# First attention of a gated two-layer block: projections and statistics one step further ahead of the scores

## The chip, the core and the metric

The kernel runs on one core of a Trainium2 chip. Its engines are called as in the profile: PE (TensorE, the matmuls; PEld is its weight load), DVE (VectorE), ACT (ScalarE), POOL (GpSimd) and SP (SyncE, which issues most DMAs). The metric is the device time of one execution in microseconds (us); the number given for the kernel is the median of three runs.

## The reference, cut to what matters

`x` is 16 batches x 128 tokens x 256. Two layers follow, each an attention and a feed-forward part added to `x` through a tanh gate. Only the first attention is touched:

```python
ln_out = _ln(layernorm(x), ln_w, ln_b)
q = _fp8_linear_pertensor(ln_out, wq, wq_scale, q_in_scale)   # 16 heads x 128
q = _ln(q per head); k = _ln(fp8 linear, 8 heads); v = fp8 linear, 8 heads
core = gqa(q, k, v)                       # softmax(q k^T / sqrt(128)) v, 2 query heads per key head
qx = _ln(fp8 linear of ln_out, per head); kx, vx = split(ctx @ w_kv_x.T); kx = _ln(kx)
xout = gqa(qx, kx, vx)
catq = fp8 rounding of concat(core, xout) / proj_smooth
x = x + tanh(g) * (catq @ wproj.T) * scale
```

Inputs of a linear are scaled, clipped and rounded to an 8-bit float. The attention is computed in two passes: self (core) for all 16 batches, then cross (xout).

## The kernel before, in words

One batch in one pass is a `Unit`: `units[0..15]` self, `units[16..31]` cross. The work of a unit is cut into four steps of four query heads each. One loop over steps n from -11 to 135 (L626) issues for each n the pieces of several units; a table of lags, written out by hand in the loop's body (L627 to L665), says which piece of which unit belongs to step n. `do(n, lag, name)` calls a piece for the head group n - lag; `once(n, step, name)` calls it once per unit, when n - step is four times the unit's number; `front(n, i)` (L619) says which of a unit's eight projection blocks (two K, four Q, two V, each 128 tokens x 512) are due in step n.

For unit u, before the change:

- `stats` (every fourth unit, L290) and `prep_norm`, `prep_tr` at 4u-8, `prep_scale`, `prep_round` at 4u-7, `prep_last` at 4u-6: layer norm of x, transposition, scaling (POOL, L366), rounding (four DVE operations at L215 to L221, last subtraction on POOL at L227), store of the rounded cross input (L388);
- `project` (PE, L410), `evict` (ACT copy to a `raw` tile, L422, or to the value tile `vt`, L419) and `bn` (DVE, L431) of blocks 0 and 1 at 4u-5, 2 and 3 at 4u-4, 4 and 5 at 4u-3, 6 and 7 (values, no `bn`) at 4u-2;
- `rstd` at 4u-2: the reciprocal deviation of all 24 heads, by four small DVE operations (L438 to L443), Ln and Exp on ACT (L175, L176), and four more on DVE (L177 to L180);
- `mult` of both K blocks and of the first Q block at 4u-2 (POOL, L454), of the other Q blocks one step later each;
- `heads` one step behind `mult`: PE transposes (L463), ACT evicts to `kT` or `qT` (L472);
- `scores` (PE, L481), `top` (DVE, L489), `exp` (ACT, L497) for head group c at 4u+c; `recip` and `divide` (DVE L505, POOL L509) one step later, `probs` (PE L517, ACT L519) two, `values` and `smooth` (PE L527, DVE L538) three, `quant` (DVE, as in `prep_round`, for two groups at once) three, `quant_last` (POOL L227) four, `output` (PE L565) five; `residual` (DVE L579) at 4u+8.

Each tile tag has a fixed number of buffers: `raw` nine, `vt` two, `qT`, `kT`, `eT` two, `e` three; a tile is reused when its last reader is done. Weights come in pieces through `load_split` and `load_kvx` on SP, at steps given by `at` (L594 to L605): the slots of the self weights are reused for the cross weights once the last self unit has been projected.

The instruction order on each engine is fixed when the program is built. A planner takes the pieces in the order of the program as priorities, with its own costs of the instructions, and lets a later piece go ahead on an engine that it holds to be idle: in the trace, all six multiplications of a unit often stand in a row on POOL, and two layer norms of the feed-forward part run at 661 and 768 us, within the first attention. [...]

Of the kernel before, what the change touches and what calls it, by code (L numbers as in the profile page):

```python
# [9 lines left out]
F32 = mybir.dt.float32  # L10
# [8 lines left out]
P = 128  # L19
B = 16  # L20
# [11 lines left out]
K_Q, K_K, K_V, K_QX = 0, 1, 2, 3  # L32
# [3 lines left out]
def flamingo_kernel(  # L36
# [197 lines left out]
    NU = 2 * B  # L234
# [4 lines left out]
    with (  # L239
# [50 lines left out]
        def stats(g):  # L290

            xg = ap.tile([P, 4, DM], F32, tag="xg", name="xg", bufs=1)
            nc.sync.dma_start(
                out=xg, in_=x_in[4 * g : 4 * g + 4].rearrange("b s d -> s b d")
            )
            mv = small.tile([P, 4, 2], F32, tag="mv0", name="mv0", bufs=2)
            for j in range(4):
                stx = small.tile([P, 6], F32, tag="st0", name="st0")
                nc.vector.bn_stats(stx, xg[:, j, :])
                nc.vector.bn_aggr(mv[:, j, :], stx)  # L300
            v1 = small.tile([P, 4], F32, tag="v1", name="v1", bufs=1)
            nc.vector.tensor_scalar(v1, mv[:, :, 1], EPS, None, ALU.add)
            r1 = rsqrt(small, v1, 4, "x1", 1)
            v2 = small.tile([P, 4], F32, tag="v2", name="v2", bufs=1)
            nc.vector.tensor_tensor(v2, r1, r1, ALU.mult)
            nc.vector.tensor_tensor(v2, v2, mv[:, :, 1], ALU.mult)
            nc.vector.tensor_scalar(v2, v2, EPS, None, ALU.add)
            r2 = rsqrt(small, v2, 4, "x2", 1)
            rr = small.tile([P, 4], F32, tag="rr", name="rr", bufs=2)
            nc.vector.tensor_tensor(rr, r1, r2, ALU.mult)  # L310
            for j in range(4):
                norms[4 * g + j] = (xg[:, j, :], mv[:, j, 0:1], rr[:, j : j + 1])

        class Unit:
# [98 lines left out]
            def evict(self, blk):  # L413
                pm = self.pm.pop(blk)
                if blk >= 6:
                    if blk == 6:
                        self.vt = ap.tile([P, 1024], F32, tag="vt", name="vt")
                    c = blk - 6
                    nc.scalar.copy(self.vt[:, c * 512 : (c + 1) * 512], pm)  # L419
                    return  # L420
                raw = ap.tile([P, 4, P], F32, tag="raw", name="raw", bufs=9)
                nc.scalar.copy(raw.rearrange("p h d -> p (h d)"), pm)  # L422
                self.raws[blk] = raw

# [166 lines left out]
        def at(n, f, *args):  # L591
            loads.setdefault(n, []).append((f, args))

        for c in range(2):  # L594
            at(-8, load_split, K_K, wkT, c)
            at(-6, load_split, K_Q, wqT, c)
            at(-5, load_split, K_Q, wqT, c + 2)
            at(-4, load_split, K_V, wvT, c)
            at(4 * B - 8 + c, load_kvx, c, 0)
            at(4 * B - 7 + c, load_split, K_QX, wqxT, c)  # L600
            at(4 * B - 6 + c, load_split, K_QX, wqxT, c + 2)
            at(4 * B - 4 + c, load_kvx, c, 1)
        for q in range(4):
            at(-2 + q // 2, load_proj, 0, q)
            at(4 * B + 2 + q, load_proj, 1, q)  # L605
# [1 line left out]
        def do(n, lag, name, *args):  # L607

            m = n - lag
            if 0 <= m < 4 * NU:  # L610
                getattr(units[m // 4], name)(m % 4, *args)

        def once(n, step, name, *args):

            m = n - step
            if m % 4 == 0 and 0 <= m // 4 < NU:
                getattr(units[m // 4], name)(*args)

        def front(n, i):  # L619

            m = n + 5
            u, step = m // 4, m % 4
            return (units[u], 2 * step + i) if 0 <= u < NU else None

        first, last = -11, 4 * NU + 7
        for n in range(first, last + 1):  # L626
            for m in range(0, B, 4):  # L627
                if n == 4 * m - 11:
                    stats(m // 4)
            once(n, -8, "load")  # L630
            for f, args in loads.get(n, ()):
                f(*args)
            ab = [front(n, i) for i in range(2)]
            do(n, 1, "recip")
            do(n, 4, "quant_last")
            do(n, 1, "divide")
            do(n, 0, "scores")
            do(n, 2, "probs")
            do(n, 0, "top")
            do(n, 0, "exp")  # L640
            if ab[0]:
                ab[0][0].project(ab[0][1])
                ab[0][0].evict(ab[0][1])
            once(n, -6, "prep_last")
            do(n, 3, "values")
            do(n, 3, "smooth")
            if ab[0]:
                ab[0][0].bn(ab[0][1])
            once(n, -2, "rstd")
            for blk in range(2):  # L650
                once(n, -2, "mult", blk)
                once(n, -1, "heads", blk)
            do(n, -2, "mult_q")
            do(n, -1, "heads_q")
            do(n, 3, "quant")
            if ab[1]:
                ab[1][0].project(ab[1][1])
                ab[1][0].evict(ab[1][1])
                ab[1][0].bn(ab[1][1])
            do(n, 5, "output")  # L660
            once(n, 8, "residual")
            once(n, -8, "prep_norm")
            once(n, -8, "prep_tr")
            once(n, -7, "prep_scale")
            once(n, -7, "prep_round")  # L665

    G = 4
    NT = G * P
# [408 lines left out]
    for g in range(B // G):  # L1077
# [3 lines left out]
        for b in range(g * G, (g + 1) * G):  # L1081
# [8 lines left out]
    ap = f2.enter_context(tc.tile_pool(name="a1", bufs=2, side="right", reuse_waits="tile"))  # L1090
    psum = f2.enter_context(
        tc.tile_pool(
            name="psum1", bufs=1, space=bass.MemoryType.PSUM, reuse_waits="tile"
# [6 lines left out]
    for n in range(-2, N1 + 5):  # L1100
# [14 lines left out]
        m = n + 2  # L1115
# [7 lines left out]
        m = n - 4  # L1123
# [5 lines left out]
    for stages in routes:  # L1129
        for _ in stages:  # L1130
# [6 lines left out]
            name="psum2", bufs=2, space=bass.MemoryType.PSUM, reuse_waits="tile"  # L1137
# [6 lines left out]
    for e in range(NE):  # L1144
# [21 lines left out]
        for c in range(NCC):  # L1166
            po = ps_sc([P, DM])
            for f in range(NFC):
# [11 lines left out]
                    ap=xe[:, c, 2 * DM + 1 : 2 * DM + 2].bitcast(I32), axis=0  # L1180
# [79 lines left out]
```

## Time and profile before

| | |
|---|---|
| median of three runs | 1548.32 us (1547.97 to 1548.7) |
| the profiled execution's own time | 1546.6 us |
| its span, first to last instruction | 1544.9 us |
| granted PE clock, mean | 0.969 |
| first scores of the first attention | at 64 us |
| self units 1 to 13 | 84.3 to 453.8 us |
| cross units 17 to 29 | 543.4 to 888.0 us |
| end of the first attention | about 948 us |
| busy over the span: PE, DVE, ACT, POOL | 90%, 68%, 53%, 43% |

The page gives for each engine its busy time and share of the span. A view by stretches gives the same for any part of the span. The list of waits says, for each group of instructions, how long its engine sat idle before it and which instruction's end ended that; the view in order of time shows the instructions with their start, length and, in brackets, the idle time before them and its releaser. The chain that ended last covers only the final scatter of this program (its longest piece is 10 us of issue at the very end), so the stages have to be read one by one.

### The profile page before, as it was taken

Reading aid. Unit: us, or ns where it says so; the run is one execution under the profiler, and the core shown is the slowest. Engines: PE = TensorE matmul, PEld = TensorE weight load, DVE = VectorE, ACT = ScalarE, POOL = GpSimd, SP = SyncE. Lnnn points to the kernel's source line nnn. Section 1 sums busy time; section 2 is a strip of 40 time slices with the busy share of each in tenths; the row PEclk is TensorE's granted clock in tenths of the full one; section 3 lists DMA queues with packets and bytes.
Section 4 is the critical chain, followed back from the end, with each engine's and each line's share of the span. In section 5 each row is a group of like instructions: output and inputs, shape, how many; then the busy total and the mean of one; then the engine's idle time right before and its main releaser. Section 6 shows DMA issues by size and latency. Waiting matters only on the chain. (4 is left out here: it accounts for less than half of the span.)

```text
span 1544.9 us, 24676 instructions
## 1 busy us (share of the span) xinstructions
PE 1395.5 (90%) x8628; PEld 1008.7 (65%) x8628; DVE 1053.4 (68%) x2789; ACT 813.6 (53%) x2420; POOL 670.8 (43%) x574
## 2 busy tenths in 40 slices
PE   2778889798888999999999987999999999996998
PEld 1567677677776677777777774555556666664887
DVE  8988878878788777776767764433579796983100
ACT  3666566566566676666666662442445554551121
POOL 4566666666666655555565654120021312111111
PEclk9799999999999999999999998999999999996999
DMA  4300001000013100000000005300210100001562
GB/s 122 112 6 23 24 11 35 12 11 21 11 45 99 45 26 16 12 21 11 18 15 18 8 8 145 104 1 0 78 54 9 49 8 36 9 36 62 191 198 70
DMA packets 50764, 68.69 MB, mean 44 GB/s; under 512 B 4939, under 2 KB 37387, under 8 KB 50640
## 3 DMA queue, kind: packets, MB, share of 16 engines
q1 hardware_dynamic: 36640, 41.31, 9.0%
q10 hardware_dynamic: 11376, 17.63, 3.5%
q0 software_dynamic: 2624, 8.16, 1.5%
q8 instruction: 69, 1.13, 0.3%
q14 instruction: 55, 0.45, 0.1%
HBM read 50.53 MB, written 16.81 MB: 44 GB/s over the span
## 5 line engine op out<-in xcount | busy, mean ns | idle before, releaser
L509 POOL TENSOR_TENSOR e<-e,sums 128x512 f32<-128x512 f32 x128 | 139.9, 1093 | 230.5 <-DVE sums L505 120.7
L497 ACT ACTIVATE e<-ps_sc,mx 128x128 f32<-128x128 f32 x512 | 181.4, 369 | 89.6 <-DVE mx L489 82.2
L454 POOL TENSOR_TENSOR raw<-raw,q_r 128x512 f32<-128x512 f32 x192 | 208.6, 1116 | 34.5 <-DVE q_r L180 33.3
L431 DVE BATCH_NORM_STATS2 q_st<-raw 128x6 f32<-128x128 f32 x768 | 173.9, 278 | 66.6 <-ACT raw L422 66.3
L1013 ACT ACTIVATE e<-ps_sc,mx 128x128 f32<-128x128 f32 x512 | 139.7, 384 | 119.7 <-DVE mx L1004 114.7
L565 PE MATMUL ps_acc<-wp,cat 128*128 128x512 f32 x512 | 160.4, 436 | 17.7 <-POOL cat L227 15.5
L463 PE MATMUL ps_tr<-ident,raw 128*128 128x128 f32 x768 | 120.7, 285 | 46.0 <-POOL raw L454 43.8
L227 POOL TENSOR_TENSOR cat<-e_t,e_e 128x1024 fp32r<-128x1024 bf16 x64 | 136.3, 2129 | 53.6 <-DVE e_t L221 53.6
L481 PE MATMUL ps_sc<-kT,qT 128*128 128x128 f32 x1024 | 138.6, 278 | 14.9 <-ACT qT L472 14.9
L481 PEld LDWEIGHTS ps_sc<-kT,qT 128*128 128x128 f32 x1024 | 129.3, 191 | 33.0 <-ACT qT L472 27.1
L463 PEld LDWEIGHTS ps_tr<-ident,raw 128*128 128x128 f32 x768 | 95.1, 146 | 82.9 <-POOL raw L454 57.9
L519 ACT COPY eT<-ps_tr 128x512 f32<-128x512 f32 x128 | 75.4, 589 | 139.5 <-PE ps_tr L517 139.4
L968 POOL TENSOR_TENSOR kb<-kT,hmask 128x512 f32<-128x512 f32 x32 | 33.6, 1069 | 250.3 <-PE ps_sc L997 188.3
L565 PEld LDWEIGHTS ps_acc<-wp,cat 128*128 128x128 f32 x512 | 95.9, 194 | 57.5 <-POOL cat L227 22.2
L527 PE MATMUL ps_pv<-eT,vt 128*128 128x256 f32 x512 | 132.1, 379 | 1.0 <-DVE cat_y L538 1.0
L422 ACT COPY raw<-ps_mm 128x512 f32<-128x512 f32 x192 | 113.8, 594 | 28.8 <-PE ps_mm L410 26.1
L527 PEld LDWEIGHTS ps_pv<-eT,vt 128*128 128x128 f32 x512 | 95.8, 189 | 31.2 <-issue 9.0
L538 DVE TENSOR_TENSOR cat_y<-ps_pv,r_sm 128x512 bf16<-128x512 f32 x128 | 87.0, 680 | 39.6 <-PE ps_pv L527 39.4
L472 ACT ACTIVATE qT<-ps_tr,hv 128x512 f32<-128x512 f32 x128 | 101.0, 789 | 21.2 <-PE ps_tr L463 19.3
L497 ACT ACTIVATION_READ_ACCUMULATOR e<-ps_sc,mx 128x1 f32 x512 | 105.6, 206 | 0.0
L489 DVE TENSOR_REDUCE mx<-ps_sc 128x4 f32<-128x512 f32 x128 | 87.2, 681 | 23.3 <-PE ps_sc L481 23.2
L1004 DVE TENSOR_REDUCE mx<-ps_sc 128x8 f32<-128x1024 f32 x64 | 78.2, 1221 | 26.1 <-PE ps_sc L997 24.5
(227 smaller groups left out, 2818.5 us busy)
## 6 DMA issues: line engine op xcount, KB each, us to landing
w1t<-in_w ACTq DMA_DIRECT2D x8, 1024.0 KB, 6.4
w2t<-in_w ACTq DMA_DIRECT2D x8, 1024.0 KB, 5.4
disp<-empty SPq DMA_DIRECT2D x16, 257.0 KB, 9.8
xe<-disp SPq DMA_DIRECT2D x8, 514.0 KB, 3.7
stage<-in_wprojT SPq DMA_DIRECT2D x16, 256.0 KB, 2.7
xg<-in_x SPq DMA_DIRECT2D x4, 512.0 KB, 3.9
xb<-in_x SPq DMA_DIRECT2D x16, 128.0 KB, 2.0
ctx<-in_ctxT SPq DMA_DIRECT2D x16, 128.0 KB, 2.2
```

What stands on the lines that cost most here:

```text
L227: nc.gpsimd.tensor_tensor(dst, t[:, part], e[:, part], ALU.subtract)
L422: nc.scalar.copy(raw.rearrange("p h d -> p (h d)"), pm)
L431: nc.vector.bn_stats(self.st[:, 4 * blk + j, :], self.raws[blk][:, j, :])
L454: nc.gpsimd.tensor_tensor(src, src, self.r[:, 4 * blk : 4 * blk + 4, None].to_broadcast([P, 4, P]), ALU.mult,)
L463: nc.tensor.transpose(pt[:, j, :], src[:, j, :], ident)
L472: nc.scalar.activation(dst, pt, AF.Identity, scale=hv[:, col : col + 1], bias=hv[:, col + 1 : col + 2])
L481: nc.tensor.matmul(pscore[:, j, :], qT[:, j, :], self.kT[:, 2 * c + j // 2, :], start=True, stop=True,)
L497: nc.scalar.activation(e[:, j, :], pscore[:, j, :], AF.Exp, bias=self.mx[:, j : j + 1], accum_out=sums[:, j : j + 1],)
L509: nc.gpsimd.tensor_tensor(e, e, sums[:, :, None].to_broadcast([P, 4, P]), ALU.mult)
L527: nc.tensor.matmul(pv[:, 2 * g : 2 * g + 2, :], self.vt[:, gg * P : (gg + 1) * P], eT[:, 2 * g : 2 * g + 2, :], start=True, stop=True,)
L565: nc.tensor.matmul(self.acc, self.cat[c // 2][:, h % 8, :], wpr[self.cross, c][:, j, :, :], start=(h == 0), stop=(h == 15),)
L1013: nc.scalar.activation(e[:, i, :], s[:, i // NQ, i % NQ, :], AF.Exp, bias=mx[:, i : i + 1])
```

## The change

Everything up to `rstd` is done one step earlier relative to the scores: `front` uses n + 6 in place of n + 5, all `prep_` pieces, `load`, `stats`, `rstd` and the weight loads of `at` move by one step, and the loop starts at -12. `mult`, `heads` and all that follows stay where they were; so do the loads of the output projection's weights (`load_proj`). Since the projected blocks and the values now live a step longer, `raw` gets eleven buffers and `vt` three: 8 KB more per partition.

```diff
-                        self.vt = ap.tile([P, 1024], F32, tag="vt", name="vt")
+                        self.vt = ap.tile([P, 1024], F32, tag="vt", name="vt", bufs=3)
...
-                raw = ap.tile([P, 4, P], F32, tag="raw", name="raw", bufs=9)
+                raw = ap.tile([P, 4, P], F32, tag="raw", name="raw", bufs=11)
...
-            at(-8, load_split, K_K, wkT, c)
-            at(-6, load_split, K_Q, wqT, c)
-            at(-5, load_split, K_Q, wqT, c + 2)
-            at(-4, load_split, K_V, wvT, c)
-            at(4 * B - 8 + c, load_kvx, c, 0)
-            at(4 * B - 7 + c, load_split, K_QX, wqxT, c)
-            at(4 * B - 6 + c, load_split, K_QX, wqxT, c + 2)
-            at(4 * B - 4 + c, load_kvx, c, 1)
+            at(-9, load_split, K_K, wkT, c)
+            at(-7, load_split, K_Q, wqT, c)
+            at(-6, load_split, K_Q, wqT, c + 2)
+            at(-5, load_split, K_V, wvT, c)
+            at(4 * B - 9 + c, load_kvx, c, 0)
+            at(4 * B - 8 + c, load_split, K_QX, wqxT, c)
+            at(4 * B - 7 + c, load_split, K_QX, wqxT, c + 2)
+            at(4 * B - 5 + c, load_kvx, c, 1)
...
-            m = n + 5
+            m = n + 6
...
-        first, last = -11, 4 * NU + 7
+        first, last = -12, 4 * NU + 7
...
-                if n == 4 * m - 11:
+                if n == 4 * m - 12:
                     stats(m // 4)
-            once(n, -8, "load")
+            once(n, -9, "load")
...
-            once(n, -6, "prep_last")
+            once(n, -7, "prep_last")
...
-            once(n, -2, "rstd")
+            once(n, -3, "rstd")
             for blk in range(2):
                 once(n, -2, "mult", blk)
                 once(n, -1, "heads", blk)
...
-            once(n, -8, "prep_norm")
-            once(n, -8, "prep_tr")
-            once(n, -7, "prep_scale")
-            once(n, -7, "prep_round")
+            once(n, -9, "prep_norm")
+            once(n, -9, "prep_tr")
+            once(n, -8, "prep_scale")
+            once(n, -8, "prep_round")
```

## The prediction

> **What bounds the kernel now.** I read the page's engine shares first, then the busy times by stage, then the first attention's stage unit by unit, then PE's waits in it, last the order of time around one of them. (A unit is one batch in one of the two passes of the first attention: 16 self units, 16 cross units, four steps n each; "step 0" below is a step with n % 4 = 0 and so on; unit u is scored at n = 4u to 4u+3.)
>
> ```profile
> PE 1395.5 (90%) x8628; PEld 1008.7 (65%) x8628; DVE 1053.4 (68%) x2789; ACT 813.6 (53%) x2420; POOL 670.8 (43%) x574
> ```
>
> PE is the engine to fill. The share is a mean, though; by stage (columns: stretch, length, then busy time and count of PE, PEld, DVE, ACT, POOL, then granted clock, DMA share, GB/s):
>
> ```profile
> 84.30:453.80 369.50, 316.66 (x1786) 264.67 (x1785) 301.45 (x842) 221.06 (x684) 248.29 (x198) 0.96 0.07 21
> 543.40:888.00 344.60, 340.86 (x1765) 253.71 (x1764) 250.01 (x732) 223.67 (x682) 197.73 (x156) 1.00 0.06 16
> ...
> 227.10:254.20 27.10, 23.58 (x139) 19.76 (x139) 22.05 (x61) 16.91 (x52) 19.03 (x16) 1.00 0.05 16
> 254.20:283.50 29.30, 25.25 (x139) 20.97 (x139) 25.22 (x76) 17.31 (x54) 19.36 (x16) 0.94 0.11 32
> ```
>
> The first row is self units 1 to 13: 369.5 / 13 = 28.42 us each, PE idle for 52.8 us in all. The second is the cross units: PE is busy 340.9 of 344.6, so nothing can be won there. The last two are single self units: one at full clock with 23.58 us of PE work, one at 0.94 with 25.25. Who ended PE's idle time in the self units:
>
> ```profile
> PE ps_tr L463 <- POOL raw L454: 38.1, 22, 3.8
> PE ps_sc L481 <- ACT qT L472: 12.0, 13, 1.7
> PE ps_acc L565 <- POOL cat L227: 2.7, 1, 2.7
> ```
>
> These three are all of the 52.8. The first is 2.93 us per unit: the head transposes wait for POOL's multiplication by the reciprocal deviation. In order of time, unit 10:
>
> ```profile
> 356.27 1.16 PE L481 MATMUL ps_sc<-kT,qT 128*128 128x128 f32 x8 [0.69 <-ACT qT L472]
> ...
> 357.71 2.12 POOL L227 TENSOR_TENSOR cat<-e_t,e_e 128x1024 fp32r<-128x1024 bf16 x1
> ...
> 357.82 2.05 DVE L178 TENSOR_TENSOR q_a<-q_a,q_var 128x24 f32<-128x24 f32 x1
> ...
> 360.12 0.18 DVE L180 TENSOR_TENSOR q_r<-q_r,q_a 128x24 f32<-128x24 f32 x1
> 360.22 0.68 DVE L489 TENSOR_REDUCE mx<-ps_sc 128x4 f32<-128x512 f32 x1
> 360.39 6.04 POOL L454 TENSOR_TENSOR raw<-raw,q_r 128x512 f32<-128x512 f32 x6 [0.55 <-DVE q_r L180]
> ...
> 361.00 0.37 ACT L497 ACTIVATE e<-ps_sc,mx 128x128 f32<-128x128 f32 x1 [2.25 <-DVE mx L489]
> ...
> 361.48 0.66 PE L463 MATMUL ps_tr<-ident,raw 128*128 128x128 f32 x4 [2.49 <-POOL raw L454]
> ```
>
> The chain of `rstd` (four DVE operations, Ln and Exp on ACT, four DVE operations) ends at 360.30, POOL starts at once, and PE, idle since 358.99, follows one multiplication later. Scores, values and projections were ready. So the wait is one of lead: `rstd` sits in the step in which its result is used.
>
> **The change part by part.** *Lead of `rstd` (front m = n+6, `rstd` at -3, `mult` and `heads` left at -2 and -1).* `rstd` gets one step (28.42 / 4 = 7.1 us) of distance to `mult`. The longest wait on raw was 3.8 us, so all of 38.1 us is covered: **-38.1**. If the cover fails by x us per unit, that is what remains of 2.93.
>
> *Clock.* Of units 1 to 13, eight have 0.94 and five 1.00; 316.7 - 13 x 23.6 = 9.9 us of PE's work is lower clock. [...] by the rows it wins up to 9.9. The rows decide, but some waits will stay: half, **-5**.
>
> *What DVE does in which step.* Nothing is added, but the work moves. From the unit's rows: every step has recip 0.17, top 0.68, smooth 0.68; bn of two blocks 2 x 0.87; `quant` 0.43 + 0.49 + 0.41 + 0.67 = 2.0; `prep_round` 2.0; residual 0.94; `prep_norm` with `prep_tr`'s two 1.2; `rstd` 8 x 0.17 = 1.4, and what it is held. Held how long is in this row (self units, mean of the one multiplication; the shortest of its kind took 0.16):
>
> ```profile
> L178 DVE TENSOR_TENSOR q_a<-q_a,q_var 128x24 f32<-128x24 f32 x15 | 26.8, 1785 | 0.4
> L438 DVE TENSOR_TENSOR q_dif<-q_st 128x24 f32<-128x24 f32 x15 | 16.8, 1123 | 0.0
> ```
>
> With L177 and L440 it makes about 3.3 us per unit. DVE per step, before: 7.4, 5.3, 8.2 (with `rstd`), 3.3; after: 8.2 (`prep_round` comes to `quant` and residual), 6.2 (`rstd`), 5.3, 4.5. Both sum to 24.2. PE needs 23.6 / 4 = 5.9 per step. So DVE falls behind by 8.2 + 6.2 - 11.8 = 2.6 us by the top of step 2, and behind DVE's top waits exp on ACT, behind exp the eviction of qT, behind that the next scores on PE. That loop took 4.4 us (scores at 338.7, qT done at 343.2), so 1.5 us is slack and 1.1 us per unit comes back as a wait of the scores for qT: **+14**. Its ends: 0 (ACT may take qT before exp, as the trace does at 347.68), and 2.93 per unit or somewhat more.
>
> [...] L178 above ends 0.04 us after `cat` does. `rstd` now lies in step 1, where POOL has `cat` 2.1, divide 1.0, xs and xx 2.3 and one multiplication 1.0: 6.5 us in a step of 5.9, never free. [...] by the rows three or four were, for 3.3 in all. I keep the rows, since POOL was as busy (6.5) in step 2 before.
>
> *`prep_scale`, `prep_last` on POOL* move with the front: POOL per step goes from 2.1, 6.1, 6.5, 4.2 to 4.0, 6.5, 4.2, 4.2. In step 2 the multiplications no longer queue behind xs and xx: already counted. *The third value tile* takes away an ACT wait (vt for ps_pv, 9.2 us in 84 to 454); ACT is busy 60% and the exp behind it was late by 0.2 us at most: 0, bound -3. *Eleven raw tiles* keep the reuse distance at one step or more (block 5 needs block 0 of the unit before, released a step earlier): 0; were a copy to wait, it would show on ACT. *DMAs* (ctx and xx loads, the xqx store, weight pieces, the loads of x for `stats`) are issued a step earlier on SP; the queues were busy 2 to 19% in these units: 0. *8 KB more SBUF* move the addresses of the tiles opened next: the load of wg was issued at 948.5, when the attention had ended, and its matmuls began at 954.0: between -6 and +1, take 0.
>
> *Fill and drain.* One more step before the first scores: two blocks' bn on DVE, which is busy 55.9 of the first 64.7 us, 1.7, rounded to **+2**; at the end one more step without projections, where PE has 4.4 us of work against a chain of 5.2: **+1**. Ends 0 and +7, a whole step.
>
> *Units 0 and 14 to 16* had 3.3 us of raw waits among weight loads: **-1**.
>
> Sum: -38.1 - 5 + 14 + 3 - 1 = -27. The profiled execution took 1546.6 (span 1544.9), which becomes 1519.5; the median of the runs, 1548.3, is 1.7 above it: **1521**.
>
> **The rivals.** *Everything goes (0.14).* ACT's order hides DVE's lag: units at 23.6 + 0.9 for qT: 13 x 3.9 = 51, less 3: 1500. For it: the cross units run so, PE 99%. Against it: there DVE is at 73%, here it would be at 90% or more.
>
> [...] POOL's 19.1 us per unit (248.3 / 13) and DVE's three rounding chains of 2.0 with `rstd`'s 1.4, 7.4 in all, exclude each other: 26.5, with handovers some 27. For it: L178 above; against it: the chains' first steps at 355.2 and 355.7 kept their length. Then 13 x 1.4 = 18, less 3: 1533.
>
> *The wait only changes its name (0.10).* Six multiplications in a row (6.04 us) still stand before a divide, and probs wait where heads did: 1548, within 3.
>
> *Slower (0.13).* DVE's two full steps fall together with longer holds: if `rstd` in step 1 is held for 6.5 us instead of 3.3, the lag at top is 5.8, the wait of the scores 4.3 per unit, 56 us, against 43 won, with 3 of fill: 1564. It decides from a wait of about 3.1 us per unit on.
>
> **How the numbers follow.** The forecast has 0.46: its own range, from the ends of the qT wait and the clock, is 1508 to 1535. Faster by over 0.2% (what a measurement of this kernel can tell from no change, 3.1 us): 0.46 + 0.14 + 0.17 = 0.77; within: 0.10; slower: 0.13. The range to hold 8 in 10: below 1502 lies half of the first rival (0.07), above 1551 the slower one (0.13).
>
> **What would show it.** Right: PE's wait for POOL raw under 5 us between the first and last self units, self units of 25.5 to 27 us, scores waiting for qT 20 to 30 us in all, fewer units at 0.94, cross units still at 26.5. Wrong: raw waits remain (the order on POOL or DVE was not moved); probs or output waiting for POOL; exp waiting for mx by over 6 us per unit; `rstd`'s DVE operations longer than 3.3 us over their 1.4; cross units above 27.

## The result, and the profile after

| | before | after |
|---|---|---|
| median of the runs | 1548.14 us (4 runs) | 1582.81 us (1581.12 to 1584.94, 4 runs) |
| ratio, 95% interval | | 1.023 (1.0218 to 1.0242) |
| profiled execution, its span | 1546.6, 1544.9 us | 1581.65, 1580.0 us |
| granted PE clock, mean | 0.969 | 0.960 |

The change makes the kernel 2.3% slower; 1521 was forecast, and the range ended at 1551. The 35.1 us between the two spans, taken apart by the starts of `top` (a unit runs from the `top` of its first step to that of the next unit): first top 64.7 → 63.2 us (-1.5), unit 0 +3.9, self units 1 to 13 +12.6, units 14 to 16 +2.8, cross units 17 to 29 +20.9, the rest -3.6.

The engine shares of the changed kernel:

```profile
PE 1410.4 (89%) x8628; PEld 1023.6 (65%) x8628; DVE 1085.8 (69%) x2789; ACT 803.2 (51%) x2420; POOL 675.9 (43%) x574
```

DVE has the same instructions as before and is busy 32 us longer: its operations last longer. By stretches (columns as before: self units 1 to 13, cross units 17 to 29, then self units 10 and 7):

```profile
86.80:468.80 382.00, 327.19 (x1787) 270.36 (x1786) 327.89 (x848) 219.03 (x686) 257.71 (x199) 0.95 0.06 20
561.20:926.70 365.50, 341.55 (x1766) 259.02 (x1765) 254.59 (x731) 218.10 (x681) 192.40 (x156) 0.99 0.05 15
352.30:380.00 27.70, 24.01 (x140) 19.77 (x139) 23.49 (x62) 16.58 (x52) 19.70 (x16) 1.00 0.05 15
261.00:293.60 32.60, 27.73 (x150) 23.32 (x150) 30.20 (x79) 17.50 (x56) 19.68 (x15) 0.92 0.09 29
```

A self unit takes 382.0 / 13 = 29.39 us (28.42 before): PE's idle time, 52.8 us before, is now 54.8, and its busy time grows by 10.5, at a lower clock. A cross unit takes 28.11 (26.50): there PE now idles for 24 us where it idled for 3.7. A plain unit at full clock (unit 10) lost only 0.6 us, unit 7 lost 3.4. PE's waits in self units 1 to 13:

```profile
PE ps_tr L463 <- ACT kT L472: 26.3, 11, 2.5
PE ps_sc L481 <- ACT qT L472: 12.8, 15, 2.8
PE ps_mm L410 <- POOL xs L227: 8.5, 12, 1.3
PE ps_acc L565 <- POOL cat L227: 7.0, 5, 2.1
```

and in the cross units:

```profile
PE ps_tr L463 <- ACT kT L472: 22.7, 13, 2.1
```

The wait for POOL raw (38.1) is gone, as forecast. In its place the same head transposes wait for ACT to empty a transpose bank. (The bank, tag `tr`, has two buffers; `prep_tr` and `probs` use it too.) Unit 10 in order of time, first the end of step 0 and step 1, then step 2:

```profile
358.05 2.14 POOL L227 TENSOR_TENSOR cat<-e_t,e_e 128x1024 fp32r<-128x1024 bf16 x1 [1.68 <-DVE e_t L221]
...
358.68 1.80 DVE L216 TENSOR_SCALAR e_e<-in_y 128x1024 uint16<-128x1024 uint16 x1
...
361.12 0.68 DVE L489 TENSOR_REDUCE mx<-ps_sc 128x4 f32<-128x512 f32 x1
...
364.17 1.20 PE L410 MATMUL ps_mm<-wk,xs 128*128 128x512 f32 x4 [0.65 <-POOL xs L227]
...
367.18 7.08 POOL L454 TENSOR_TENSOR raw<-raw,q_r 128x512 f32<-128x512 f32 x6 [0.77 <-DVE q_r L180]
...
369.67 1.07 DVE L216 TENSOR_SCALAR e_e<-cat_y 128x1024 uint16<-128x1024 uint16 x1
...
370.86 1.06 DVE L220 TENSOR_SCALAR e_e<-e_e 128x1024 bf16<-128x1024 bf16 x1
...
373.68 0.67 DVE L489 TENSOR_REDUCE mx<-ps_sc 128x4 f32<-128x512 f32 x1
...
374.44 0.37 ACT L497 ACTIVATE e<-ps_sc,mx 128x128 f32<-128x128 f32 x1 [2.23 <-DVE mx L489]
...
375.83 1.46 ACT L472 ACTIVATE kT<-ps_tr,hv 128x512 f32<-128x512 f32 x2
...
376.76 0.63 PE L463 MATMUL ps_tr<-ident,raw 128*128 128x128 f32 x4 [2.51 <-ACT kT L472]
```

Two things are to be seen. At 358.68 the input's rounding (L216 on `in_y`) starts beside `cat` and takes 1.80 us, until 0.29 us after `cat` has ended (0.42 before the change). At 367 POOL's six multiplications, started earlier than before, lie across `quant`: L216 and L220 take 1.07 and 1.06 us for 0.43 and 0.41, and end where a multiplication does (7.08 / 6 = 1.18 us each, so at 370.7 and 371.9). The `top` behind them comes 3.5 us after its scores (made from 369.06 to 370.22), the exp behind `top`, and the eviction of kT, already possible at 373.3, behind exp. So the bank that PE waits for comes back late at the end of a chain that begins with POOL's row. The late `top` is only in part new: in the mean of units 1 to 13 it comes 4.54 us after the first score of its step, and 3.98 before the change, and the first kT has left its bank 7.47 us after that score (7.43 before). What is new is that PE, which no longer waits for raw, is at the head transposes 2.2 us sooner. In cross unit 27 this chain is all that is left:

```profile
856.43 6.21 POOL L454 TENSOR_TENSOR raw<-raw,q_r 128x512 f32<-128x512 f32 x6 [0.77 <-DVE q_r L180]
...
861.77 1.15 DVE L216 TENSOR_SCALAR e_e<-cat_y 128x1024 uint16<-128x1024 uint16 x1
...
864.06 1.18 PE L410 MATMUL ps_mm<-wq,xx 128*128 128x512 f32 x4
...
865.52 0.67 DVE L489 TENSOR_REDUCE mx<-ps_sc 128x4 f32<-128x512 f32 x1
...
868.14 1.48 ACT L472 ACTIVATE kT<-ps_tr,hv 128x512 f32<-128x512 f32 x2
869.09 0.63 PE L463 MATMUL ps_tr<-ident,raw 128*128 128x128 f32 x4 [1.42 <-ACT kT L472]
```

The same place in the kernel before:

```profile
826.75 1.88 PE L410 MATMUL ps_mm<-wxk,ctx 128*128 128x512 f32 x4
...
827.69 0.68 DVE L489 TENSOR_REDUCE mx<-ps_sc 128x4 f32<-128x512 f32 x1
...
830.31 1.48 ACT L472 ACTIVATE kT<-ps_tr,hv 128x512 f32<-128x512 f32 x2
...
831.27 0.63 PE L463 MATMUL ps_tr<-ident,raw 128*128 128x128 f32 x4
```

There the eviction stood behind exp as well, and PE had more to do meanwhile: the step had the cross K blocks' projections (`wxk`, 1.88 us for four matmuls), which the change has moved a step ahead; now it has Q blocks (1.18). In the mean of units 17 to 29, counted from the first score of the step, the first kT has left its bank at 6.45 us (5.73 before), and PE is ready for the third transposes at 4.86 (5.80). Of the 1.66 us by which their wait grew (0.08 to 1.74), 0.72 are the later `top` and 0.94 the shorter projections.

Where DVE is held shows in the groups of the self units (busy us, then the mean of one in ns); before:

```profile
L178 DVE TENSOR_TENSOR q_a<-q_a,q_var 128x24 f32<-128x24 f32 x13 | 26.0, 2001 | 0.3
L220 DVE TENSOR_SCALAR e_e<-e_e 128x1024 bf16<-128x1024 bf16 x39 | 17.3, 443 | 0.2
L216 DVE TENSOR_SCALAR e_e<-cat_y 128x1024 uint16<-128x1024 uint16 x26 | 11.7, 448 | 0.1
L216 DVE TENSOR_SCALAR e_e<-in_y 128x1024 uint16<-128x1024 uint16 x13 | 5.5, 422 | 0.1
```

and after:

```profile
L220 DVE TENSOR_SCALAR e_e<-e_e 128x1024 bf16<-128x1024 bf16 x39 | 25.9, 664 | 0.0
L216 DVE TENSOR_SCALAR e_e<-in_y 128x1024 uint16<-128x1024 uint16 x13 | 22.0, 1690 | 0.0
L216 DVE TENSOR_SCALAR e_e<-cat_y 128x1024 uint16<-128x1024 uint16 x26 | 17.9, 690 | 0.2
L178 DVE TENSOR_TENSOR q_a<-q_a,q_var 128x24 f32<-128x24 f32 x13 | 2.4, 181 | 0.4
```

L178 of `rstd` no longer lies beside `cat` (it saves 23.6 us; L438, 1268 ns in the mean, stays at 1252), and the rounding chains pay instead (in_y alone 16.5, the other two rows 14.8).

Not every self unit lost. Of the 12.6 us, units 3 and 7 have 6.7 (29.2 → 32.6 each), unit 13 has 2.2, the other ten 3.7 together. Units 3 and 7 run `stats` of later batches, earlier than before; in unit 3:

```profile
165.69 3.48 POOL L454 TENSOR_TENSOR raw<-raw,q_r 128x512 f32<-128x512 f32 x3
...
168.22 0.97 DVE L178 TENSOR_TENSOR x_a<-x_a,v 128x4 f32<-128x4 f32 x1
...
169.13 2.13 POOL L227 TENSOR_TENSOR cat<-e_t,e_e 128x1024 fp32r<-128x1024 bf16 x1
169.22 2.06 DVE L179 TENSOR_SCALAR x_a<-x_a 128x4 f32<-128x4 f32 x1
```

L179 takes 2.06 us for four elements per partition, to the end of `cat`.

### The profile page after: what moved, and what is told of

The parts are those of the page before. It is cut to its first block, busy times and chain, and to the rows that moved or that the text cites. A ratio compares the mean times of both kernels' runs of the same rounds, so it can differ in the third digit from the quotient of the medians.

```text
span 1580.0 us, 24617 instructions
## 1 busy us (share of the span) xinstructions
PE 1410.4 (89%) x8628; PEld 1023.6 (65%) x8628; DVE 1085.8 (69%) x2789; ACT 803.2 (51%) x2420; POOL 675.9 (43%) x574
## 5 line engine op out<-in xcount | busy, mean ns | idle before, releaser
L431 DVE BATCH_NORM_STATS2 q_st<-raw 128x6 f32<-128x128 f32 x768 | 177.0, 279 | 80.3 <-ACT raw L422 79.2
L454 POOL TENSOR_TENSOR raw<-raw,q_r 128x512 f32<-128x512 f32 x192 | 213.1, 1143 | 28.9 <-DVE q_r L180 27.3
L565 PE MATMUL ps_acc<-wp,cat 128*128 128x512 f32 x512 | 166.9, 451 | 19.8 <-POOL cat L227 19.5
L463 PE MATMUL ps_tr<-ident,raw 128*128 128x128 f32 x768 | 116.0, 281 | 55.6 <-ACT kT L472 54.0
L481 PEld LDWEIGHTS ps_sc<-kT,qT 128*128 128x128 f32 x1024 | 138.2, 199 | 35.4 <-ACT qT L472 27.1
L481 PE MATMUL ps_sc<-kT,qT 128*128 128x128 f32 x1024 | 143.7, 285 | 15.4 <-ACT qT L472 15.3
L565 PEld LDWEIGHTS ps_acc<-wp,cat 128*128 128x128 f32 x512 | 99.4, 200 | 63.3 <-POOL cat L227 25.9
L1004 DVE TENSOR_REDUCE mx<-ps_sc 128x8 f32<-128x1024 f32 x64 | 78.2, 1221 | 26.1 <-PE ps_sc L997 23.8
```

The costliest lines, as they stand in the source:

```text
L431: nc.vector.bn_stats(self.st[:, 4 * blk + j, :], self.raws[blk][:, j, :])
L454: nc.gpsimd.tensor_tensor(src, src, self.r[:, 4 * blk : 4 * blk + 4, None].to_broadcast([P, 4, P]), ALU.mult,)
L463: nc.tensor.transpose(pt[:, j, :], src[:, j, :], ident)
L481: nc.tensor.matmul(pscore[:, j, :], qT[:, j, :], self.kT[:, 2 * c + j // 2, :], start=True, stop=True,)
L565: nc.tensor.matmul(self.acc, self.cat[c // 2][:, h % 8, :], wpr[self.cross, c][:, j, :, :], start=(h == 0), stop=(h == 15),)
```

## The experiments

My first theory was that all of the loss is the bank given back behind exp behind a late `top` (A in the texts on record). Against it stood that DVE has too much work in its full steps, whatever POOL does (B, later D); that ACT itself is what makes kT late; and, later, that there are two costs, the bank in the cross units and, in the self units, DVE held by POOL (theory P; the P of the table is a run). All times are medians, each ratio is against the kernel before on the same chip (1546.1 to 1549.4 us), with its 95% interval; "self" is the mean of units 1 to 13, "cross" of 17 to 29, "held" the time of DVE's operations above the 5th percentile of their kind in that run, per self unit.

| kernel | time, us | ratio (interval) | self | cross | held |
|---|---|---|---|---|---|
| before | 1548.14 | 1 | 28.42 | 26.50 | 5.24 |
| after | 1582.81 | 1.023 (1.0218–1.0242) | 29.39 | 28.11 | 7.00 |
| heads_first (H) | 1563.86 | 1.0095 (1.0075–1.0115) | 29.42 | 26.88 | 7.95 |
| mult_paced (M) | 1566.33 | 1.0112 (1.0095–1.0129) | 29.24 | 27.12 | 7.36 |
| prep_early (P) | 1552.59 | 1.003 (1.0022–1.0039) | 26.94 | 28.11 | 5.66 |
| first_paced (H, M) | 1559.22 | 1.007 (1.0053–1.0087) | 29.26 | 26.60 | 8.71 |
| heads_prep (H, P) | 1546.13 | 1.000 (0.9989–1.001) | 27.77 | 26.77 | 4.72 |
| paced_prep (M, P) | 1534.35 | 0.992 (0.9898–0.9943) | 27.06 | 27.10 | 5.82 |
| all_three (H, M, P) | 1533.87 | 0.9903 (0.9884–0.9922) | 27.10 | 26.75 | 4.18 |
| kt_dve | 1608.43 | 1.0383 (1.0366–1.04) | 31.24 | 27.95 | 8.00 |
| mult_quarter | 1507.12 | 0.9732 (0.9709–0.9755) | 26.99 | 25.96 | 5.65 |
| bn_quarter | 1574.96 | 1.017 (1.0146–1.0193) | 30.38 | 26.46 | 6.92 |
| prep_only | 1562.15 | 1.0099 (1.0082–1.0117) | 29.34 | 26.46 | 7.01 |
| rstd_only | 1545.84 | 0.9989 (0.998–0.9998) | 27.42 | 26.95 | 4.03 |
| rstd_three | 1568.30 | 1.0129 (1.0104–1.0154) | 29.79 | 26.97 | 4.96 |
| round_early | 1573.73 | 1.0175 (1.0152–1.0197) | 28.82 | 28.12 | 5.61 |
| three_round | 1553.45 | 1.0042 (1.0026–1.0058) | 28.59 | 26.76 | 6.65 |

**heads_first (H)**, on the changed kernel:

```diff
             do(n, 2, "probs")
+            for blk in range(2):
+                once(n, -1, "heads", blk)
             do(n, 0, "top")
...
-                once(n, -1, "heads", blk)
```

> The changed kernel, with the two K blocks' head transposes issued ahead of top and exp of their step, so that on ACT the eviction of kT comes before exp (all but the second one wholly so). Theory A (PE waits because three head blocks of one step share two transpose banks, and the first two are given back by ACT only after exp, which waits for a late top): the heads' wait for ACT kT falls from 54 us to under 10, cross units go from 27.7 back to about 26.5 us, plain self units from 27.7 to about 25.5; 1535 us, between 1520 and 1550. Theory B (DVE has too much in too few steps since the lead was moved, the kT wait is only where it shows): the wait moves to the scores (for qT) or to probs, 1570 to 1585 us.

Measured: the wait for the bank is gone in both stages, and the cross units have most of their loss back (28.11 → 26.88; 26.50 before the change). The self units did not move: their largest wait is now another one.

```profile
PE ps_acc L565 <- POOL cat L227: 34.4, 13, 3.1
```

So the order around the bank was what cost in the cross units, and in the self units only the place where a lag showed.

**mult_paced (M)**: `behind` adds an edge that only orders: each multiplication stands behind the `divide` of its step, so that POOL runs 3, 1, 1, 1 instead of six in a row (code shortened).

```diff
-                nc.gpsimd.tensor_tensor(
+                ins = nc.gpsimd.tensor_tensor(
                     src, src, self.r[...].to_broadcast([P, 4, P]), ALU.mult,
                 )
+                if pool_last:
+                    behind(ins, pool_last[0])   # pool_last: the step's divide
```

> The changed kernel, with each of POOL's multiplications kept behind the divide of its step, so that they stand 3, 1, 1, 1 instead of six in a row; the order on DVE, ACT and PE stays nearly as it was. Theory A1 (top is late in step 3 because DVE's rounding chain is held, operation by operation, by POOL's row of six multiplications): the chain's three operations fall from 1.07, 1.06 and 1.32 us towards 0.45, 0.42 and 0.7, top comes 1 to 2 us earlier, the heads' wait for ACT kT falls to half or less; 1550 us, between 1535 and 1565. Theory A2 (the order on ACT alone, exp ahead of kT, is enough for the wait): kT wait within 20% of 54 us, 1575 to 1590. Theory B (DVE's load by step): no more than 10 us gained.

Measured: cross 27.12 without touching the head transposes, the wait for kT there 22.7 → 7.9 us. So the row on POOL is at the head of that chain. What is left fits the shorter projections: `top` now comes 1.88 us after the first score, sooner than before the change (2.26), and the transposes still wait 0.61. The self units again stay, and so does their wait for kT (26.1).

**kt_dve**: the eviction of kT on DVE in place of ACT (`tensor_scalar`, two scalars, for blocks 0 and 1).

> The changed kernel, with kT written from the transpose bank by DVE instead of ACT, which takes it out of ACT's queue behind exp; on DVE it stands behind the same top. Theory A: the bank is free one exp (1.5 us) earlier, so the wait falls from about 2.5 to about 1 us per self unit and from 1.5 to about 0 per cross unit; 1550 us, between 1535 and 1565. Theory B (DVE's load): 1.4 us more DVE work per unit makes self units longer, 1585 to 1600.

Measured: slower still, beyond both answers, with DVE busy 27.5 us per self unit. In the cross units the transposes still wait, 18.4 us, now for DVE. So taking the eviction out of ACT's queue gives little there; in the self units the added DVE work hides what it might give.

**first_paced**: H and M together.

> Both: K heads ahead of exp, and the multiplications paced. Theory A: if both causes are links of one chain, the second adds little to the first: 1520 to 1540 us, no more than 12 us better than the better one of the two. If they are separate costs, the gains over the changed kernel add up. Theory B: 1570 or more.

Measured: cross 26.60, as before the change; self 29.26, where the wait has moved to the residual's output bank (1.80 per unit). The bank-and-exp theory thus fits the cross units and explains none of the loss in the self units.

**mult_quarter** leaves out the scaling of three of a block's four heads on POOL, **bn_quarter** the statistics of three of four on DVE; both results are therefore not the block's, and only their times are of use.

> The changed kernel, with POOL's multiplication done on one of a block's four heads (the scaling of the other three is left out): 3 to 4.5 us less POOL work per unit, all waits kept. Theory P [...]: DVE's held time falls from 7.0 us per self unit to 4.5 or less, self units from 29.4 to 27 or less; cross units to 26.6 or less, since the rounding chain isn't held any more; 1520 to 1540 us. Theory D (DVE has too much own work in neighbouring steps): held time falls, but self units stay within 1 us of 29.4; 1555 to 1575 us.

> The changed kernel, with the statistics of one of a block's four heads (the other three are set to a constant): some 4 to 5 us less DVE work per unit, of a kind that POOL doesn't hold. Theory P: DVE is held as long as before (6 us or more per self unit) and self units stay at 28 us or more; cross units keep the wait for kT, 27.5; 1565 to 1585 us. Theory D: self units fall to 26.5 or less and the wait for kT shrinks by half, as top comes earlier; 1525 to 1545 us.

Measured: with POOL at 15.3 us per unit instead of 19.8, self units of 26.99, though held time fell only to 5.65 (4.5 or less was expected); the shorter multiplications also free POOL sooner for `divide`, `cat` and `xs`, which this run can't part from the holds. With three quarters of DVE's statistics gone (DVE 22.1 instead of 25.2), 30.38, though the holds stayed at 6.9. (The statistics are of a kind that POOL was not seen to hold: L431 took 268 to 298 ns in units 1 to 29 of the changed kernel.) DVE's total work is not what bounds the self units, then. The second run also reorders DVE (the rounding L220 took 1.15 us in the mean there, 0.66 in the changed kernel), so it excludes the simple form of that theory and no more.

**prep_early (P)**, on the changed kernel:

```diff
-            once(n, -7, "prep_last")
+            once(n, -8, "prep_last")
...
-            once(n, -9, "prep_norm")
-            once(n, -9, "prep_tr")
-            once(n, -8, "prep_scale")
-            once(n, -8, "prep_round")
+            once(n, -10, "prep_norm")
+            once(n, -10, "prep_tr")
+            once(n, -9, "prep_scale")
+            once(n, -9, "prep_round")
```

> The changed kernel, with the five input preparation pieces one more step ahead, so that the input rounding no longer falls into the step of quant and residual: DVE's work per step would be 6.2, 6.2, 6.5, 5.3 us instead of 8.2, 6.2, 5.3, 4.5. Theory D: self units fall from 29.4 to 28 or less, the wait for POOL xs (9.9 us) goes; cross units unchanged at 27.7 to 28.1; 1555 to 1567 us. Theory P: held time stays near 7 us per self unit and the units at 29 or more; 1572 to 1590 us.

Measured: 30 us back, more than either answer had, all of it before the cross units: self 26.94, cross units as in the changed kernel to 0.01 us. L216 on in_y is back at its own length (L220 is held longer instead, 1.06 us in the mean, and held time falls to 5.66 in all):

```profile
L216 DVE TENSOR_SCALAR e_e<-in_y 128x1024 uint16<-128x1024 uint16 x12 | 5.1, 427 | 0.0
```

**all_three**: H, M and P together, and **heads_prep**: H and P.

> K heads ahead of exp, multiplications paced, and preparation one more step ahead, together. Theory D: self units 27.5 or less, cross units 26.6, 1525 to 1540 us, the first version below the kernel before. Theory P: self units stay at 29 or more with DVE held for 8 us, 1552 to 1562 us.

> The changed kernel with the head transposes and their evictions ahead of the step's top and exp, and the input's scaling, rounding and store one more step ahead; the order of the multiplications on POOL stays as the change made it (without the pacing of the version that has all three). If the two costs of the change (the transpose bank given back behind exp, and the input's rounding in the step of the quantisation) are all there is, pacing adds nothing: 1534 to 1540 us, self units at 27.1 or less, cross units at 26.9, so that 0.15 us per cross unit (2 us) is all that pacing gives. If the row of six multiplications on POOL costs by itself, this is 5 us or more behind the version with all three: 1540 to 1548, self units at 27.5 or more, with output waiting for POOL.

Measured: all_three beats the kernel before by 1.0%. Its two stages:

```profile
86.40:438.70 352.30, 311.66 (x1790) 254.85 (x1789) 292.97 (x850) 219.54 (x687) 251.47 (x198) 1.00 0.07 22
528.20:876.00 347.80, 343.23 (x1770) 257.68 (x1769) 249.60 (x732) 216.64 (x682) 190.70 (x156) 0.99 0.06 16
```

The mean clock of the self units is at 1.00. Without pacing (heads_prep) 12 us of that are gone: of the two answers on record it was the second, that the row costs by itself, but not through the wait that I had named. The head transposes wait 28.9 us for DVE's eviction of the transposed input from the same bank (15.6 with pacing), the output for POOL only 3.2.

**prep_only**: the kernel before, with the five input pieces alone moved one step ahead (-7, -9, -9, -8, -8).

> The kernel before, with nothing changed but that layer norm, scaling, rounding and store of the input go one step further ahead (projections, statistics of the heads and multiplications as before). If the raw wait of the kernel before (38 us) comes from rstd standing in the step of its use, it stays, the self units remain at 28.0 to 28.6 and the time is 1545 to 1552. If it comes from DVE and POOL being late with the input's rounding, so that rstd starts late, most of it goes without any change to the projections' lead: self units under 27.3 and 1530 to 1538. Cross units stay at 26.5 in both cases.

Measured: neither of the two answers. The raw wait nearly stays (34.9 us in units 1 to 13, 38.1 before), and the kernel becomes 15 us slower. The self units cost 29.34 with 7.01 held, the changed kernel's 29.39 and 7.00, and the same operation is held:

```profile
L216 DVE TENSOR_SCALAR e_e<-in_y 128x1024 uint16<-128x1024 uint16 x13 | 22.0, 1690 | 0.0
```

Cross units are untouched (26.46). This is the self units' loss on its own: the pieces land in step 0, where `quant` and the residual are. It puts their work and their holds there together; no run takes the holds away and leaves DVE's work and order as they are, so how much of the 0.92 us is which stays open.

**rstd_only** and **rstd_three**: the kernel before with `rstd` moved to the end of step -3 (`once(n, -3, "rstd")` after the second `bn`); rstd_three adds H and M.

> The kernel before, with nothing changed but that rstd comes at the end of the step in which its last statistics are made, not in the next one; projections, statistics and input rounding keep their places. If the lead of rstd is what the raw wait is about, it falls from 38 us to under 15, self units to 27.0 to 27.7, 1533 to 1543. If moving rstd brings POOL's multiplications forward onto the quantisation's last step as the change did, the wait of heads for the transpose bank appears here too, cross units rise to 27 or more, and the time is 1548 to 1565 although the projections were not moved.

> The kernel before with rstd at the end of the step in which its last statistics are made, the head transposes ahead of the step's top and exp, and the multiplications ordered behind the step's divide on POOL; projections, statistics, input rounding and the buffers are those of the kernel before. If the projections' extra step of lead is not needed (its only use being to let rstd go earlier), this does as well as the version that has all three on the changed kernel: 1525 to 1537, self units 26.7 to 27.3, cross units 26.5 to 26.8, and first scores at 63 us and not 67. If the lead of the projections itself carries a part of the gain (rstd alone left 1.86 us per unit of waits for the multiplications, because the last statistics come late in its step), the raw wait stays at 1.5 us or more, self units at 27.5 or more, and the time is 1538 to 1548.

Measured: rstd alone takes a full microsecond per self unit (raw wait in all 43.8 → 24.2), and gives it back in cross units (+0.45 each), units 14 to 16 (+1.5 each) and behind them: 0.1% in all (interval 0.02 to 0.2%). The wait for kT, which the second answer had expected in the cross units, is 2.1 us there and not 22.7: `top` comes 2.43 us after the first score (3.02 in the changed kernel), and with the projections in their old place PE is ready for the third transposes only at 5.81 us (4.86). With H and M on top it is slower, the raw wait at 38.0 in all: the multiplications wait for the step's `divide`. So the early `rstd` by itself shortens the raw wait, and pacing (tried here only with H) pays on the changed kernel and not on this one; that the projections' lead is what gives it the room is my reading, not shown.

**round_early, paced_prep, three_round**: of P only scaling, rounding and store moved; M with P; H and M with that part of P.

> The changed kernel with only the input's scaling, rounding and store one more step ahead, out of the step of quantisation and residual; layer norm and transposition stay where the change put them. If it is the rounding (four DVE operations and two on POOL meeting the quantisation's four) that costs, the self units come down to 27.0 to 27.4 as with all five pieces moved, cross units stay at 28.1, first scores come at 63 to 66 us: 1548 to 1556. If layer norm and transposition are the ones that lie badly, self units stay at 28.8 or more and the time at 1573 to 1583.

> The changed kernel with the multiplications ordered behind the step's divide on POOL and the five input pieces one more step ahead; head transposes stay behind top and exp. If the two remedies are independent, it takes off both what pacing took alone (1583 to 1566: 16) and what the input pieces took alone (1583 to 1553: 30): 1536, self units at 26.9, cross units at 27.1 as with pacing alone. If the row of six multiplications is what stands in the way of both, it is as good as the version that has all three, 1534 or less; if the head transposes' place is needed too, it stays at 1542 or more.

> The version that has all three remedies, with layer norm and transposition left where the change put them (only scaling, rounding and store go one more step ahead). In the version with all three, head transposes waited 15.6 us for the transposed input to leave its bank; if that comes from layer norm and transposition standing in the step of the query heads' transposes, it goes, self units fall to 26.3 and first scores come at 64 us: 1520 to 1528. If the rounding, now directly behind the transposition in one step, comes late for the projections instead, they wait for its last subtraction by 1 us per unit or more and the time is 1533 to 1545.

Measured: paced_prep equals all_three within the intervals, so beside M and P the place of the head transposes adds nothing that can be told. round_early fell on its second answer, three_round on neither: rounding alone gives 0.57 of P's 2.44 us per unit. Plain units such as unit 10 take 27.3 us (changed kernel 27.7, prep_early 26.1), and units 3 and 7 stay at 31.2 and 33.2 (prep_early 27.3): only with all five pieces does the planner also run `stats` two steps earlier in unit 3. In order of time, unit 9 to 10 of round_early:

```profile
346.05 2.00 POOL L366 TENSOR_TENSOR in_y<-lnT,r_in 128x1024 bf16<-128x1024 f32 x1 [1.32 <-DVE lnT L356]
...
350.71 1.64 POOL L227 TENSOR_TENSOR xs<-e_t,e_e 128x768 fp32r<-128x768 bf16 x1 [2.66 <-DVE e_t L221]
351.32 1.30 DVE L215 TENSOR_SCALAR cat_y<-cat_y 128x1024 bf16<-128x1024 bf16 x1
```

The scaling has to wait for the transposition of the same step, so the input's last subtraction still reaches into `quant`, whose first operation takes 1.30 us for 0.42. In prep_early both subtractions are over (at 331.24) before `quant` begins (at 331.62). That this is what plain units lack is read from the trace, not tried by itself.

## Why the prediction was wrong

**Raw wait, -38.1: right.** 0.2 us of it is left between 60 and 950 us. It says only that one name has gone; the idle time of PE in the self units went from 52.8 to 54.8.

**What DVE does in which step, +14: the step that failed.** PE's idle time in the self units that was no raw wait went from 14.7 to 54.8 us: 40 us, not 14. I summed DVE's work per step with `quant` and `prep_round` at 2.0 us each, their free lengths, and let only `rstd` be held ("I keep the rows"). The direction of DVE's lag was right: step 0, from top to top, went from 7.19 to 8.85 us in unit 10. But the holds moved with the work. `rstd` in step 1, where I put the risk, was held less than before (L178 181 ns in the mean for 2001, L438 1252 for 1268); `prep_round` in step 0 was held beside `cat` for 1.27 us, and `quant` by the multiplications, which the early `rstd` had set free to run earlier. The rows that I kept belonged to the old neighbours, and the trace before had a warning: in its cross units the multiplications held `quant` already.

```profile
L220 DVE TENSOR_SCALAR e_e<-e_e 128x1024 bf16<-128x1024 bf16 x32 | 32.6, 1018 | 0.5
```

prep_only shows the part of `prep_round` in this term: 0.92 us per self unit, and none of the gain. Much of the rest, as I read the trace, is a lag that the raw wait had covered: PE comes to the head transposes 2.2 us sooner and finds the bank full, and `top` was late in that step before the change too. I had also named the wrong loop: the wait for qT hardly changed (12.0 → 12.8), kT's bank, xs and cat took the time (41.8 us together).

**Clock, -5: wrong in sign.** PE's busy time rose by 10.5 us, at 0.95. The idle time came back at once, and as before mostly in single waits: 15 of 1.8 to 2.8 us (before 14 of 2.5 to 3.9). Nine of the 13 units had a mean clock of 0.88 to 0.95 (last section).

**Cross units, 0: wrong, 20.9 us, the largest term.** "PE is busy 340.9 of 344.6, so nothing can be won there" left out what can be lost. The cross units have `rstd`, the multiplications and two `quant`s too, and what hid the eviction behind exp was the cross K blocks' projections, which the change moved away. I had checked the buffers that the change enlarges and not the one that it uses at another time, the two transpose banks.

**`stats` a step earlier, not costed: 6.7 us** in units 3 and 7, as I read the trace; no run moves `stats` alone. I priced the issue of its loads and not its small DVE operations.

**Fill and drain, +3.** First scores came 1.5 us earlier, unit 0 took 3.9 more, the rest 3.6 less: -1.2, just below the ends given (0 and +7).

**Units 14 to 16, -1:** +2.8, again waits for kT and cat.

**The rivals.** The slower one (1564) had the right sign and too small a price: DVE held longer at its two full steps, but by the rounding chains, not by `rstd`. The one of 1533 (0.17), in which POOL's work and DVE's chains exclude each other, had a part of what the trace shows (159 of 183 held operations end with one of POOL, last section) and priced it at 27 us per unit, for self units only. "The wait only changes its name" was right about PE's idle time in the self units (52.8 → 54.8 us), though it named `probs` and not the bank. From the trace before I had taken L178, up to 2.05 us, ending 0.04 us after `cat`. The trace after has others at such lengths: in the self units L216 on in_y took up to 1.80 us (0.42 at its shortest), L220 up to 1.97 (0.40), and L179 in `stats` 2.06 on four elements (0.15). What decides whether an operation is held no trace here shows. My reading is that every rounding operation that can lie beside a POOL operation was at risk, and that is what had to be laid out step by step.

## What to carry to other kernels

An operation's length in the profile holds for the neighbours that it had: before moving work by a step, list what it will stand beside (on the banks it uses, in the order on its engine, and on an engine whose operations held it in the trace), and use the held length where such a neighbour comes (here L216 on in_y: 422 ns in the mean before the change, 1690 beside `cat`). A stage that runs at 99% has nothing to win and everything to lose; ask of each moved piece whether it runs there too, and which wait it covered where it stood. Moving a whole front by one step moves a good piece and a bad one together: here the early `rstd` was good for the self units and the input's rounding bad, and with the input moved one step further still and POOL's row split up the change gains 1%.

## What the runs showed of the hardware

Whether a single wait of PE of some 2 us went with a lower clock depended here on when it fell. In the changed kernel's cross units one wait of 2.11 to 2.15 us (units 17, 21, 25) went with a granted clock of 0.94 and a unit of 29.5 to 30.5 us; one of 1.73 to 1.76 (units 18, 22) with 1.00 and 27.7. In the self units a wait of 2.5 went with 0.94 in units 6 and 8 and with 1.00 in 9 and 10. The records of the granted clock in the traces before and after have two values, 1.0 and 0.5, and in each of the two all changes lie on one grid of 3.413 us, to 0.001 us. I counted how long PE was idle in each full-clock step of that grid between 64 and 950 us of these two traces: after 2.0 us or more the next step was at half clock in all 20 cases, after less than 1.6 us in none of 450, and in between in 6 of 21. Counted so, 2.04 and 2.05 us of the wait lay in one step in units 6 and 8; in units 9 and 10 a step began in the middle of it (1.91 and 0.59; 1.52 and 0.99). (The ends of matmuls are modelled in the profile, so the limit is no sharper than that.)

A held DVE operation showed no idle time and no releaser here (L216 on in_y: 1690 ns in the mean, 0.0 us of idle time before all 13): it is merely long, and ends close to the end of a POOL operation (within 0.3 us for 159 of the 183 that were held by over 0.3 us in units 1 to 29 of the changed kernel). Held time therefore counts as busy in the shares (DVE 1053 → 1086 us with the same instructions) and appears in no list of waits; here it was found by comparing the mean of a group with its shortest member.
